# Global attention in steps of three half-column passes over six score banks

## The chip, the core and the metric

The kernel runs on one core of a Trainium2 chip. The metric is the device time of one execution in microseconds; the median of several runs is compared. Engines are named as the profile names them: PE is TensorE's matrix multiply, PEld its weight load, DVE is VectorE, ACT is ScalarE, POOL is GpSimd, SP is SyncE, which issues most transfers.

## The reference, cut to what matters

For each of 8 images of 64 x 64 tokens with 256 channels, two layers follow each other. The first is attention in windows of 512 tokens, 4 heads of 32 in horizontal windows (channels 0 to 127) and 4 in vertical ones (channels 128 to 255), plus a depthwise 3 x 3 convolution. The second is attention over all 4096 tokens with one head of 32; the change is in that one.

```python
# layer 2, tokens xf of one image, N = 4096, d = 32
f = xf @ kf + bf
g = xf @ kg + bg
h = xf @ kh + bh
s = jnp.einsum('bnd,bmd->bnm', g, f)
beta = jax.nn.softmax(s, axis=-1)
v = jnp.einsum('bnm,bmd->bnd', beta, h)
o = v @ kv + bv
out = gamma[0] * o.reshape(B, H, W, C) + x
```

## The kernel before, in words

**Units and steps.** The work is a list of units: per image 8 horizontal windows (`h0` to `h7`), 8 vertical ones (`v0` to `v7`) and two global units (`l0`, `l1`), each of which treats half of the queries as four blocks of 512. The first horizontal unit of the next image stands ahead of the two global units. A window unit has 4 steps, a global unit 32, one for each block of 128 keys (a tile).

One step does, for four blocks at once: scores, exponential, values, sum.

- `scores(c)` (L860 in global units, L679 in windows): four matmuls with 32 rows each, one in each row group of TensorE, 128 keys by 512 queries. The matmuls are fp32 and each stands as two instructions in the trace. The outputs are two bank pairs `s` of `[128, 2, 512]`, that is four PSUM banks. Three pairs exist, and `sc_tiles` hands out two of them in turn, so that one pair is free when the next step begins.
- `weights_of` (L477): two exponentials on ScalarE, one per pair, into the weights `p_l` (tag `pt`, three buffers).
- `weighted(c)` (L876): four matmuls, one in each column group, add into `num_l`. It is issued one step later, behind the next step's scores.
- `add(c)` (L887): VectorE adds the weights into `acc_l`, `[128, 4, 512]`; after the last step a matmul with ones (`sums`, L896) makes the denominators, `norm` (L904) divides and `result` (L915, and L262 through `product`) makes the output, which L925 evicts.

**Filler.** Between values and the next scores TensorE is given other work in half-width pieces: the projections of the next image (`pq`, L262), `pf` and `phd` for the global layer, and sums. VectorE and ScalarE have filler too: the convolution's taps (L618 on ScalarE, the other eight L622 on VectorE), evictions, hard-swish (L597, L604) and transposes.

**Order.** All of it stands in an order made by a planner (`Flow`) while the program is built. It keeps a clock for TensorE, ScalarE, VectorE and SyncE from fixed costs, and picks tasks by due times (`DUE`, in steps relative to a unit). Each engine then runs its own list in that order, and waits on semaphores. SyncE's list holds the loads of `x`, the round trips `kvia` and `via_v` through DRAM, and the outputs.

**GpSimd.** It has little to do: `clip` clears the border of an image part `hv` (L589 to L595) and `swish` copies two halo rows between neighbours (L609, L610).

A second program path with exact maxima stands behind a test of the denominators and is not taken with these inputs.

Of the kernel before, what the change touches and what calls it, by code (L numbers as in the profile page):

```python
# [18 lines left out]
P = 128  # L19
C = 256  # L20
H = W = 64
N = H * W
# [9 lines left out]
def quad(r):  # L32
# [3 lines left out]
HALVES = 2  # L36
QH = 4

DUE = dict(
    near_k=-4, near_q=-3, near_values=-13, clip=-2, swish=4,  # L40
    conv_h0=13, conv_h1=10, conv_h2=7, conv_h3=16, conv_v0=-3, conv_v1=-3, conv_v2=14, conv_v3=9,
    tap=-5, join_h=14, join_hl=10, join_v=12, context=0, norm=2, release=0, sums=-2, add=1, adds_h=0, adds_v=0, add2=1, apart=4,
    fg0=-7, fg2=11, fg3=20, h0=3, h1=14, values_v=-3, near0=3, spread0=12, spread1=61,
    conv_first=-10, far_swish=1,
# [7 lines left out]
SCORES, VALUES, PROD, TURN, DRAIN = 0.96, 0.88, 0.86, 0.65, 0.11  # L52
# [3 lines left out]
ISSUE, LOAD, VIA, FETCH, HALO = 0.6, 4.3, 2.6, 2.8, 2.6  # L56
# [20 lines left out]
class Flow:  # L77
# [5 lines left out]
    def __init__(self):  # L83
        self.t = 0
        self.clock = dict(pe=0.0, act=0.0, dve=0.0, sp=0.0)
        self.lanes = dict(pe=[], turn=[], act=[], dve=[], sp=[], res=[])
        self.open = None
        self.held = None
        self.bank_free = 0.0
        self.half_end = self.exp_end = 0.0  # L90
        self.apart = 0
# [116 lines left out]
    def step(self, scores, values):  # L208
        c = self.clock
        self.apart += 1  # L210
# [8 lines left out]
        if scores:  # L219
            scores()  # L220
            c["pe"] = max(c["pe"] + DRAIN, self.half_end + LAG) + SCORES
            self.half_end = max(c["act"], c["pe"] + PE_LAG) + EXP
# [12 lines left out]
        if self.held:  # L235
            self.held()
            c["pe"] = max(c["pe"] + DRAIN, before + LAG) + VALUES
        self.held = values
# [4 lines left out]
        for task in self.waiting("sp"):  # L243
            if task.begin() <= self.clock["pe"] + 0.5:
                self.run(task)
# [20 lines left out]
def tile_attention_blocks(  # L266
# [19 lines left out]
    B = xT.shape[0]  # L286
    PSUM = bass.MemoryType.PSUM
# [115 lines left out]
    seen = [const.tile([P, 2 * NB + 2, TB // D], F32, name=f"seen{i}") for i in range(2)]  # L403
    for t in seen:
        nc.gpsimd.memset(t, 1.0)

    def attention(images, load_x, out_rows, exact):


# [21 lines left out]
        pairs = cycle([ps_sc.tile([P, 2, TB], F32, name=f"s_{i}") for i in range(3)])  # L431
# [36 lines left out]
        def sc_tiles():  # L468
            return [next(pairs), next(pairs)]
# [49 lines left out]
        def image(b):  # L519
# [8 lines left out]
            def note():  # L528
                for t, op in zip(seen, (ALU.max, ALU.min)):
                    nc.vector.tensor_tensor(t, t, recs(), op)  # L530
# [50 lines left out]
            def clip(i, half):  # L581


                if i % 2 == 0:
# [4 lines left out]
                    nc.gpsimd.memset(v[:, :, 0:1], 0.0)  # L589
                    nc.gpsimd.memset(v[:, :, W + 1 : W + 2], 0.0)  # L590
                v = hv[i // 2, half]
                if i == 0:
                    nc.gpsimd.memset(v[:, 0, :], 0.0)
                if i == NB - 1:
                    nc.gpsimd.memset(v[:, 17, :], 0.0)  # L595
# [5 lines left out]
            def swish(i, half):  # L601
# [4 lines left out]
                )  # L606
                if i and i % 2 == 0:
                    here, before = hv[i // 2, half], hv[i // 2 - 1, half]
# [222 lines left out]
            def global_unit(z):  # L831
# [22 lines left out]

                def scores(c):
                    if exact and c == 0:
                        maxima()
                    sc = sc_tiles()
                    for r in range(NQ):
                        nc.tensor.matmul(  # L860
                            row_of(sc, r), lhsT=f4[quad(r), c * P : (c + 1) * P],
                            rhs=gq[quad(r), z, :], start=True, stop=not exact,
                        )
                        if exact:
                            row = slice(r * D, r * D + 1)
                            nc.tensor.matmul(
# [467 lines left out]
```

## Time and profile before

| | us |
|---|---|
| median of 3 runs | 3437.23 (3435.89 to 3438.12) |
| the profiled execution's own time | 3432.03 |
| its span, first to last instruction | 3430.1 |
| TensorE busy | 3368.3 (98%) |
| VectorE busy | 2729.4 (80%) |
| ScalarE busy | 2666.5 (78%) |
| GpSimd busy | 63.1 (2%) |
| granted TensorE clock | 0.997 |

In time, one image takes about 421 us: some 227 us of window units and 194 us of global units, in the middle of the run. Busy time of TensorE counts a matmul from its start to a modelled end, and an instruction that waits inside a group of matmuls isn't seen as idle time; starts are the firmer measure. Columns of a timeline: start, length, engine, line, operation, output and inputs, shape, count, and in brackets the idle time before it and what ended that.

### The profile page before, as it was taken

How to read it: one execution, taken by the hardware profiler on the slowest of the kernel's cores; microseconds unless marked ns; L12 is line 12 of the kernel's file. 1: busy time of each engine (PE TensorE's matmuls, PEld its weight loads, DVE VectorE, ACT ScalarE, POOL GpSimd, SP SyncE). 2: the span in 40 equal slices, each digit the busy share in tenths (PEclk: the TensorE clock that was granted, in tenths of full speed). 3: DMA queues.
4: the chain of work that ended last, by engine and by line, in shares of the span. 5: the costliest groups of instructions: out<-in, count | busy, mean ns of one | idle time of the engine just before them, and what ended most of it. 6: DMA issues, size and time to landing. Idle time of an engine off the chain costs nothing.

```text
span 3430.1 us, 80125 instructions
## 1 busy us (share of the span) xinstructions
PE 3368.3 (98%) x34804; PEld 1154.6 (34%) x34804; DVE 2729.4 (80%) x2276; ACT 2666.5 (78%) x3235; POOL 63.1 (2%) x266
## 2 busy tenths in 40 slices
PE   8999999999999999999999999999999999999997
PEld 3333333333333333333333333333333333333322
DVE  4897798777897778968789687896878968788776
ACT  5788777887787877878778787787877878778875
POOL 0000000000000000000000000000000000000000
PEclk9999999999999999999999999999999999999998
DMA  2131103311123111231112311123111231122200
GB/s 71 57 99 51 56 28 88 96 46 50 44 72 100 48 45 44 72 106 41 50 50 75 98 37 47 56 81 92 40 38 59 84 86 40 38 72 65 70 31 26
DMA packets 249417, 209.94 MB, mean 61 GB/s; under 512 B 26080, under 2 KB 190432, under 8 KB 249056
## 3 DMA queue, kind: packets, MB, share of 16 engines
q1 hardware_dynamic: 246816, 204.18, 20.4%
q8 instruction: 275, 4.51, 0.6%
q10 hardware_dynamic: 2240, 0.56, 0.1%
q14 instruction: 86, 0.70, 0.1%
HBM read 99.78 MB, written 83.89 MB: 54 GB/s over the span
## 4 chain that ended last, share of the span: by engine, by line
PE 79%; DVE 14%; ACT 4%; issue 2%; DMA 1%; DVEq 0%; ACTq 0%; SPq 0%
PE s L679 16%; DVE acc_l L887 12%; PE pq L262 11%; PE s L860 10%; PE num_l L876 8%; PE num_v L696 7%; PE num_h L696 7%; PE s L262 6%; PE sum_h L714 5%; PE sum_v L714 5%; PE pf L783 2%; DVE act L622 1%; ACT p_l L477 1%; ACT p_h L477 1%; PE s L915 1%
## 5 line engine op out<-in xcount | busy, mean ns | idle before, releaser
L887 DVE TENSOR_TENSOR acc_l<-acc_l,p_l 128x2048 f32<-128x2048 f32 x480 | 1099.8, 2291 | 230.7 <-ACT p_l L477 207.6
L477 ACT ACTIVATE p_l<-s 128x1024 f32<-128x1024 f32 x1024 | 992.9, 1026 | 200.6 <-PE s L860 143.7
L622 DVE SCALAR_TENSOR_TENSOR act<-hv,dw_sb,act 128x1024 f32<-128x1024 f32 x512 | 655.7, 1281 | 22.7 <-ACT act L618 8.6
L860 PE MATMUL s<-gq,f 32*128 32x512 f32 x4096 | 625.9, 640 | 1.4 <-ACT ot_l L925 0.9
L477 ACT ACTIVATE p_h<-s 128x1024 f32<-128x1024 f32 x512 | 494.5, 1023 | 94.9 <-PE s L679 70.9
L477 ACT ACTIVATE p_v<-s 128x1024 f32<-128x1024 f32 x512 | 496.0, 1023 | 92.7 <-PE s L679 86.9
L876 PE MATMUL num_l<-p_l,h_sb 128*32 128x512 f32 x4096 | 546.4, 605 | 2.4 <-ACT nums_l L891 2.1
L262 PE MATMUL pq<-x,wqkv_sb 128*32 128x256 f32 x8192 | 524.0, 382 | 2.1 <-ACT qh L551 0.8
L262 PEld LDWEIGHTS pq<-x,wqkv_sb 128*32 128x32 f32 x8192 | 261.3, 110 | 368.9 <-issue 201.9
L679 PE MATMUL s<-qh,kh 32*128 32x512 f32 x2048 | 319.0, 641 | 10.3 <-ACT qh L551 5.9
L679 PE MATMUL s<-qv,kv 32*128 32x512 f32 x2048 | 317.7, 640 | 0.2 <-ACT p_v L477 0.2
L860 PEld LDWEIGHTS s<-gq,f 32*128 32x128 f32 x4096 | 192.9, 182 | 298.6 <-issue 284.7
L696 PE MATMUL num_v<-p_v,vs 128*32 128x512 f32 x2048 | 272.7, 605 | 2.5 <-DMA vs<-kvia 2.5
L696 PE MATMUL num_h<-p_h,vs 128*32 128x512 f32 x2048 | 271.6, 602 | 3.5 <-ACT nums_l L891 1.9
L262 PE MATMUL s<-act,wout_sb 128*32 128x512 f32 x2048 | 227.0, 595 | 0.0
L925 ACT ACTIVATE ot_l<-s,bias_o 128x512 f32<-128x512 f32 x128 | 81.2, 684 | 174.2 <-PE s L262 162.7
L876 PEld LDWEIGHTS num_l<-p_l,h_sb 128*32 128x32 f32 x4096 | 80.7, 108 | 387.5 <-issue 370.7
L705 DVE TENSOR_TENSOR acc_h<-p_h,p_h 128x2048 f32<-128x2048 f32 x64 | 146.5, 2290 | 44.1 <-ACT p_h L477 30.9
L705 DVE TENSOR_TENSOR acc_v<-p_v,p_v 128x2048 f32<-128x2048 f32 x64 | 146.6, 2291 | 36.8 <-ACT p_v L477 36.8
L679 PEld LDWEIGHTS s<-qh,kh 32*128 32x128 f32 x2048 | 97.1, 183 | 182.2 <-issue 146.7
L679 PEld LDWEIGHTS s<-qv,kv 32*128 32x128 f32 x2048 | 101.6, 182 | 162.2 <-issue 157.9
L714 PE MATMUL sum_h<-p_h,ones 128*32 128x256 f32 x2048 | 137.3, 380 | 4.2 <-ACT kv L570 4.2
(125 smaller groups left out, 2417.8 us busy)
## 6 DMA issues: line engine op xcount, KB each, us to landing
x<-in_xT SPq DMA_DIRECT2D x92, 512.0 KB, 3.9
kvia<-kt SPq DMA_DIRECT2D x128, 256.0 KB, 2.4
vs<-kvia SPq DMA_DIRECT2D x512, 64.0 KB, 2.1
out<-ot_l SPq DMA_DIRECT2D x128, 256.0 KB, 2.1
via_v<-nums_v SPq DMA_DIRECT2D x64, 256.0 KB, 2.1
shuf_v<-via_v SPq DMA_DIRECT2D x256, 64.0 KB, 2.0
f<-fg SPq DMA_DIRECT2D x256, 64.0 KB, 2.0
gq<-fg SPq DMA_DIRECT2D x64, 64.0 KB, 2.0
```

What stands on the lines that cost most here:

```text
L262: nc.tensor.matmul(out[quad(r), :], lhsT=lhsT[:, quad(r)], rhs=rhs, start=start, stop=stop)
L477: nc.scalar.activation(pt[:, 2 * z : 2 * z + 2, :], sc[z], AF.Exp, scale=scale)
L622: nc.vector.scalar_tensor_tensor(o, src, wt, o, ALU.mult, ALU.add)
L679: nc.tensor.matmul(row_of(sc, r), lhsT=k[quad(r), c * P : (c + 1) * P], rhs=q[quad(r), :], start=True, stop=not exact,)
L696: nc.tensor.matmul(u["num"][quad(r), :], lhsT=vs[kind, i][:, r, c, :], rhs=u[c][:, r, :], start=(c == 0), stop=(c == 3),)
L705: nc.vector.tensor_add(u["acc"], u["acc"] if c == 2 else u[0], u[c])
L714: nc.tensor.matmul(u["sum"][quad(r), cols], lhsT=ones[:, :D], rhs=pt[:, r, cols], start=(k == 0), stop=(k == len(of) - 1),)
L783: nc.tensor.matmul(pf[quad(r), cols], lhsT=wcomb[:, k, quad(r % 2)], rhs=act_of(2 * p + r // 2, k, cols), start=(k == 0), stop=(k == 1),)
L860: nc.tensor.matmul(row_of(sc, r), lhsT=f4[quad(r), c * P : (c + 1) * P], rhs=gq[quad(r), z, :], start=True, stop=not exact,)
L876: nc.tensor.matmul(u["num"][quad(r), :], lhsT=h_sb[:, c, :], rhs=u[c][:, r, :], start=(c == 0), stop=(c == 4 * NB - 1),)
L887: nc.vector.tensor_add(u["acc"], u["acc"], u[c])
L925: nc.scalar.activation(ot, po, AF.Identity, bias=bias_o[:, m : m + 1])
```

## The change

The first two tiles of a global unit keep the old step. The other 30 are treated as 60 half-column passes, a pass being one tile against one half (256) of the query columns, and three passes make a step: 2 + 20 steps in place of 32. A step takes all three bank pairs: `first`, `mid` and `last`. Row groups 0 and 1 write `first` in passes one and two and `mid` in pass three; row groups 2 and 3 write `mid` in pass one and `last` in passes two and three. The next step gets the pairs in the order first, last, mid.

The pair `mid` is so written by different row groups in passes one and three. Between them stands a hand-over: an empty GpSimd instruction waits for pass one's last matmul, and pass three's first matmul waits for that instruction.

Three exponentials follow, the third (`mid`) into a tile `pm` of its own with one buffer. Values are three passes of four matmuls. VectorE adds twice per step, `add` for four half pairs and `add_rest` for `mid`.

The borders and halo copies of `hv` become tasks of their own (`edges`) in a new GpSimd lane, placed when VectorE's part is at least `BEHIND` = 3.0 us past by the planner's clock. Due times are set anew, some orders between tasks are changed, and the notes on denominators (`seen`) are kept per image.

```diff
 DUE = dict(
-    near_k=-4, near_q=-3, near_values=-13, clip=-2, swish=4,
-    conv_h0=13, conv_h1=10, conv_h2=7, conv_h3=16, conv_v0=-3, conv_v1=-3, conv_v2=14, conv_v3=9,
-    tap=-5, join_h=14, join_hl=10, join_v=12, context=0, norm=2, release=0, sums=-2, add=1, adds_h=0, adds_v=0, add2=1, apart=4,
-    fg0=-7, fg2=11, fg3=20, h0=3, h1=14, values_v=-3, near0=3, spread0=12, spread1=61,
-    conv_first=-10, far_swish=1,
+    near_k=-4, near_q=-2, near_values=-13, clip=6, swish=4,
+    conv_h0=12, conv_h1=10, conv_h2=6, conv_h3=18, conv_v0=-3, conv_v1=-5, conv_v2=16, conv_v3=9,
+    tap=-5, join_h=12, join_hl=13, join_v=12, context=0, norm=-6, release=0, sums=-2, add=1, adds_h=0, adds_v=0, add2=9, apart=-5,
+    fg0=-10, fg2=8, fg3=12, h0=1, h1=4, values_v=-3, near0=0, spread0=8, spread1=41,
+    conv_first=-13, far_swish=2,
 )
...
         if scores:
-            scores()
-            c["pe"] = max(c["pe"] + DRAIN, self.half_end + LAG) + SCORES
-            self.half_end = max(c["act"], c["pe"] + PE_LAG) + EXP
+            rest = scores()
+            c["pe"] = max(c["pe"] + DRAIN, self.half_end + LAG) + SCORES + more
+            self.half_end = max(c["act"], c["pe"] - more + PE_LAG) + EXP
+            if more:
+                self.half_end = max(self.half_end, c["pe"] + PE_LAG) + EXP
...
+        for task in self.waiting("pool"):
+            if task.begin() + BEHIND <= self.clock["pe"]:
                 self.run(task)
...
+                    first, mid, last = sc = [pairs.popleft() for _ in range(3)]
+                    pairs.extend((first, last, mid))
+                    for n, (tile, h) in enumerate(passes_of(c)):
+                        for r in range(NQ):
+                            mm = score(place_of(c, n, r, sc), r, tile, side(h))
+                            if n == 0 and r == 3:
+                                relay = nc.gpsimd.nop()
+                                handed(relay, mm)
+                            if n == 2 and r == 0:
+                                handed(mm, relay)
+                    pt = ptp.tile([P, NQ, TB], F32, tag="pt", name=name)
+                    nc.scalar.activation(pt[:, :2, :], first, AF.Exp)
+                    nc.scalar.activation(pt[:, 2:, :], last, AF.Exp)
+
+                    def rest():
+                        pm = ptp.tile([P, 2, TB], F32, tag="pm", name=f"{name}_m", bufs=1)
+                        nc.scalar.activation(pm, mid, AF.Exp)
+                        u[c] = pt, pm
...
+                    pt, pm = u[c]
+                    for n in (0, 2, 1):
+                        tile, h = passes_of(c)[n]
+                        for r in range(NQ):
+                            nc.tensor.matmul(
+                                u["num"][quad(r), side(h)], lhsT=h_sb[:, tile, :],
+                                rhs=place_of(c, n, r, (pt[:, :2], pm, pt[:, 2:])),
+                                start=False, stop=(c == l_steps - 1 and n == 1),
+                            )
...
+                def add_rest(c):
+
+                    h = passes_of(c)[0][1]
+                    acc = u["acc"].rearrange("p (j i) c -> p i j c", j=2)[:, :, :, side(h)]
+                    nc.vector.tensor_add(
+                        acc, acc, u[c][1].rearrange("p i (j c) -> p i j c", j=2)
+                    )
...
+                    if i % 2 == 0 or i == NB - 1:
+                        edges[i, half] = flow.add(
+                            "pool", [(partial(im.edges, i, half), [("pool", HALO)])], due, [sw[i, half]]
+                        )
...
+            def then():
+                if c - 1 in u.added:
+                    flow.require(u.added[c - 1])
+                rest()
```

## The prediction

> **What bounds the kernel now.** I read the busy table first, then the costliest groups, then the timeline of one global step with filler and of some without. From the page, parts 1 and 5:
>
> ```profile
> PE 3368.3 (98%) x34804; PEld 1154.6 (34%) x34804; DVE 2729.4 (80%) x2276; ACT 2666.5 (78%) x3235; POOL 63.1 (2%) x266
> ...
> L887 DVE TENSOR_TENSOR acc_l<-acc_l,p_l 128x2048 f32<-128x2048 f32 x480 | 1099.8, 2291 | 230.7 <-ACT p_l L477 207.6
> L477 ACT ACTIVATE p_l<-s 128x1024 f32<-128x1024 f32 x1024 | 992.9, 1026 | 200.6 <-PE s L860 143.7
> ...
> L860 PE MATMUL s<-gq,f 32*128 32x512 f32 x4096 | 625.9, 640 | 1.4 <-ACT ot_l L925 0.9
> ...
> L876 PE MATMUL num_l<-p_l,h_sb 128*32 128x512 f32 x4096 | 546.4, 605 | 2.4 <-ACT nums_l L891 2.1
> ```
>
> TensorE looks like the only bound. The timeline of an image's global stage, TensorE alone, starts of groups in the first column:
>
> ```profile
> 1624.29 1.14 PE L860 MATMUL s<-gq,f 32*128 32x512 f32 x8
> 1625.36 1.07 PE L876 MATMUL num_l<-p_l,h_sb 128*32 128x512 f32 x8
> 1626.24 1.05 PE L262 MATMUL pq<-x,wqkv_sb 128*32 128x256 f32 x16
> 1627.22 1.14 PE L860 MATMUL s<-gq,f 32*128 32x512 f32 x8
> ```
>
> Start to start, scores take 1.07 us, values 0.88 (1.00 where scores follow at once), and 16 half-width instructions of filler 0.98. Within scores the second four start 0.534 after the first four, within values 0.454; in filler each four of 256 columns take 0.216. So 512 columns take 0.427, and the rest is turning round: 0.107 of weights in the open plus 0.11 of emptying for scores, 0.027 plus 0.113 for values. A global step without filler is 2.07 us, of which 0.357 is turning.
>
> The other view, the last image's stage, where filler has run out:
>
> ```profile
> 3370.13 1.94 ACT L477 ACTIVATE p_l<-s 128x1024 f32<-128x1024 f32 x2 [0.46 <-DVE acc_l L887]
> 3370.14 9.48 DVE L887 TENSOR_TENSOR acc_l<-acc_l,p_l 128x2048 f32<-128x2048 f32 x4
> ...
> 3372.52 1.94 ACT L477 ACTIVATE p_l<-s 128x1024 f32<-128x1024 f32 x2 [0.46 <-DVE acc_l L887]
> 3373.25 0.64 PEld L860 LDWEIGHTS s<-gq,f 32*128 32x128 f32 x8 [0.84 <-issue]
> 3373.26 1.47 PE L860 MATMUL s<-gq,f 32*128 32x512 f32 x8
> ...
> 3375.65 0.64 PEld L860 LDWEIGHTS s<-gq,f 32*128 32x128 f32 x8 [0.84 <-issue]
> 3375.65 1.47 PE L860 MATMUL s<-gq,f 32*128 32x512 f32 x8
> ```
>
> Here steps start 2.40 apart, not 2.07: four dependent adds take 9.48, so one comes every 2.396 (2.292 plus 0.104 until its own result is visible), the exponentials wait for VectorE, and scores (now 1.40 long) wait inside. TensorE still counts as busy. **VectorE is the bound wherever a step has little filler.** Three weight buffers hide this for about ten tiles after filler ends; then 2.40 sets in. From starts over the whole trace I sum 135 us of such stretching: 4.8 in each of six global stages of 194.2 us, 6.2 in the seventh, 12.1 in the last, the rest mostly in window stages.
>
> **What the Trainium skill says.** "TensorE: Matmul & The Clock Gate", section "LDWEIGHTS (loading the stationary operand)", has load time go by columns, not rows: the trace agrees, 0.107 exposed for 128 columns and 0.027 for 32. "TensorEngine Tiling (Array Packing)", section "Gotcha 1: PSUM Pressure", says row tiles may not write one bank at the same time and software must order them: the reason for the hand-over; nothing run so far shows a collision. "PSUM — Partial Sum Buffer", section "Engine vs sequencer instructions", puts a nop on the sequencer alone, so the hand-over needs no GpSimd datapath, but its queue is a strict FIFO. The trace supports the price: wait-only instructions take 17 ns (ScalarE) and 21 ns (VectorE).
>
> **The change, part by part.** The order of the built program gives the counts.
>
> *Turns.* Per half image, 2 full steps and 20 of three passes replace 32, so 160 fewer score/values pairs over 16 halves: 160 x 0.357 = 57.1 us off. A 256-column pass costs 0.432 against 0.427: 320 steps x 6 passes x 0.0045 = 8.6 back. Doubled weight loads lie under streaming (0.107 against 0.216); if not, each is worth up to 0.1 us. Net 48.5 off; pricing every group in both orders gives 48.6 (51.6 in global stages, 3.0 back in window stages).
>
> *Step length.* Three passes: scores 0.107 + 6 x 0.216 + 0.11 = 1.51, values 1.44, together 2.95 us, for 1.5 tiles (3.10 before).
>
> *Adds.* Per step a 128x2048 add and a 128x1024 one. The trace's 2.292 (2048) and 0.69 (512) give 1.22 for 1024. Both are in the chain on `acc`: 2.292 + 1.22 + 2 x 0.104 = **3.72 us per step** against 1.5 x 2.396 = 3.59. That exceeds 2.95, and what lets VectorE trail shrinks: the middle pair's weights have one buffer, so the third exponential of step k waits for the second add of k-1, and (third bank pair) the second pass of k+1 waits for that exponential. All six banks belong to one step. Three exponentials, 0.92 apart, then cost nothing more: about 3.3 per step, under 3.72.
>
> *Filler.* In the new order a middle image's global stage has 11 three-pass steps without filler, 7 with 0.4 to 0.6 us, 7 with about 1.2, 13 with 1.4 to 1.9, and 2 with 9.9 (results). Taking the later of TensorE and VectorE step by step, the 11 gain 9.7 us of wait (VectorE 42.2, TensorE 32.5), the 7 gain 5.6, the rest about 4. Full-filler neighbours can absorb lateness of about 1.1 us; following it through by hand leaves 12.7 per stage, against 4.8 now: +7.9, times 7 = +55. Bounds: 4.8 (no worse than now) and 19.3 (nothing absorbed). So bare work falls 6.5 per stage and waits rise 7.9.
>
> *Last image.* 36 of its 40 three-pass steps have no filler. At 3.72 the stage takes about 165 us. Before it took 169.3 with two results tasks (16.1) inside. In the new order these two come after the last step, the normalisation feeding them standing behind the adds on VectorE. Of their 16.1, 9.3 falls into gaps where TensorE now idles (4.2 before L896, 5.1 from L896 to L915). Net 165 + 16.1 - 9.3 - 169.3 = +2.5; the turns above already count -6.1 of it, so +8.6.
>
> *Hand-over.* Row group 3 of pass one streams until 0.56 us after the step's start; a result is visible 0.21 after streaming (scores at 1624.29, exponential at 1625.46, streaming ending 0.96 in). Wait-only instruction 0.02, back to TensorE 0.05 (exponential end to weight load in the tail), weights 0.107: 0.95, and pass three may start at 0.97. Just hidden: lower bound 0; it removes no wait, so no gain. Upper, 0.15 late: 320 x 0.15 = 48. Queued behind the waiting matmul are pass three and all later TensorE work; ScalarE's second and third exponentials wait for it. I take 3.
>
> *GpSimd's queue.* Today it stands waiting for VectorE up to 165 us at a time, harmless as no engine is near it. Now a hand-over could stand behind such a copy. The new `edges` tasks are placed 3 us after planned readiness, and in global stages cost 3.35 us of GpSimd work. Taken 0; upper 20 in all.
>
> *Window stages.* Re-tuned due times move filler, taps and joins, and the DMAs of `fetch_values` and `load` with them, past others on SP. VectorE gets about 5 us more per image there (4.5 of its work moves out of the global stage). The summed later-of-TensorE-and-ScalarE rises 1.9 per stage. I take +1 x 7 = +7, from -15 to +20. The one memset fewer and the smaller `seen` reductions: nothing (VectorE slack).
>
> Sum: -48.6 + 55 + 8.6 + 3 + 7 = **+25 us**. Against the profiled execution's 3432.0 (span 3430.1 plus 1.9) that is 3457; the median of the runs is 5.2 above it, so 3462.
>
> **Rivals.**
> 1. *The banks and buffers cover it; faster.* One mechanism: in the 18 low-filler steps per stage, VectorE's lateness is taken up by filled neighbours and waits stay at 4.8 per stage. Then -48.6 plus a few: about 3391. It decides below 11.3 us of wait per stage (4.8 + 6.5). For: the present stage's later-of sum is 17 us above TensorE, yet only 4.8 is lost. Against: that relies on three buffers, and the middle pair now has one. Chance 0.26.
> 2. *Balance.* Waits come to some 10 us per stage and window stages don't grow: 3437. Chance 0.10.
> 3. *The hand-over is late.* 0.15 per step, or copies ahead of it in GpSimd's queue: 48 to 68 on top of my sum, 3510 to 3530. Chance 0.06.
> The change not doing what it says is excluded: the new order shows the half-column passes and a TensorE wait on GpSimd's sequencer in each step.
> My forecast, VectorE pacing the low-filler steps, has 0.58.
>
> **How the numbers follow.** My own case runs 3440 to 3500. The range 3405 to 3500 adds balance and the upper half of rival 1, leaving out its lower half and rival 3, about 0.2. Within 0.2% (6.9 us) is about what measurement here can't tell from no change. Faster 0.26, same 0.10, slower 0.64.
>
> **What would show it.** Right: three-pass steps without filler start about 3.7 apart, not 2.95; the third exponential waits for `acc_l`; VectorE without gaps there; global stages 195 to 199 us. Hand-over: the weight load of pass three with no wait on GpSimd, pass one to pass three 0.86 apart. Wrong: global stages near 188, or a tail below 3.4 per step, or idle time put down to GpSimd.

## The result, and the profile after

The changed kernel takes 3461.98 us (median of 4 runs, 3461.68 to 3464.65), the kernel before 3436.56 beside it: ratio 1.0077, 95% interval 1.0060 to 1.0094. The profiled execution took 3462.07 us, its span 3460.3. The forecast was 3462.0.

Lines of the page after that answer to those shown of before (line, engine, operation; busy us and mean ns; idle time before, and what ended most of it):

```profile
PE 3393.1 (98%) x42484; PEld 1519.6 (44%) x42484; DVE 2753.7 (80%) x2436; ACT 2686.8 (78%) x3235; POOL 62.9 (2%) x264
...
L983 DVE TENSOR_TENSOR acc_l<-acc_l,p_l 128x2048 f32<-128x2048 f32 x320 | 733.1, 2291 | 203.6 <-ACT p_l L947 189.5
...
L989 DVE TENSOR_TENSOR acc_l<-acc_l,p_l_m 128x1024 f32<-128x1024 f32 x320 | 392.1, 1225 | 33.5 <-DVE acc_l L983 0.5
L951 ACT ACTIVATE p_l_m<-s 128x1024 f32<-128x1024 f32 x320 | 329.2, 1029 | 74.2 <-DVE acc_l L989 70.6
```

480 additions of 2.29 us have become 320 of 2.29 and 320 of 1.225: per tile VectorE now has more to do. The third exponential, L951, waits 70.6 us in all for the middle addition. The waits of the whole trace (us, times, longest) show who passes this on:

```profile
PEld s L901 <- ACT p_l_m L951: 89.7, 198, 2.5
...
ACT p_l_m L951 <- DVE acc_l L989: 70.6, 155, 1.8
...
PEld s L901 <- ACT p_l L947: 41.1, 99, 0.8
```

In the trace of before, weight loads of the global scores waited 7.0 us for exponentials in all. The timeline of one step without filler, late in an image's global stage (start, length):

```profile
895.79 2.36 PE L901 MATMUL s<-gq,f 32*128 32x256 f32 x24
895.94 1.02 ACT L951 ACTIVATE p_l_m<-s 128x1024 f32<-128x1024 f32 x1 [0.44 <-DVE acc_l L989]
895.95 2.29 DVE L983 TENSOR_TENSOR acc_l<-acc_l,p_l 128x2048 f32<-128x2048 f32 x1
...
897.02 0.73 PEld L901 LDWEIGHTS s<-gq,f 32*128 32x128 f32 x12 [0.50 <-ACT p_l_m L951]
...
898.35 1.23 DVE L989 TENSOR_TENSOR acc_l<-acc_l,p_l_m 128x1024 f32<-128x1024 f32 x1
...
899.51 2.37 PE L901 MATMUL s<-gq,f 32*128 32x256 f32 x24
899.67 1.02 ACT L951 ACTIVATE p_l_m<-s 128x1024 f32<-128x1024 f32 x1 [0.44 <-DVE acc_l L989]
```

VectorE runs L983, L989, L983 with 0.10 us between them. The third exponential starts 0.09 us after L989 ends, and the second half of pass two starts when that exponential has freed its bank. Scores last 2.29 us to the first values instead of 1.51, and the step 3.72 instead of 2.95.

By place, from the starts of the global scores (us; "middle" is the median of the seven stages before the last, from first to last scores; "windows" is the sum of the seven stretches between global stages; "tail" runs from the last scores to the end). These columns come from each kernel's one profiled execution, which lay 4.5 us under the median for before and 10.4 under it for e3_no_triples:

| kernel | median | first global stage begins | middle | windows | last stage | tail |
|---|---|---|---|---|---|---|
| before | 3436.6 | 285.6 | 193.7 | 1577.3 | 168.2 | 41.6 |
| after | 3462.0 | 294.1 | 195.8 | 1578.1 | 169.7 | 47.2 |
| e1_buffer | 3466.0 | 296.3 | 192.9 | 1603.0 | 171.1 | 41.9 |
| e2_narrow | 3412.8 | 295.1 | 191.1 | 1579.1 | 153.2 | 46.9 |
| e3_no_triples | 3498.0 | 295.9 | 193.7 | 1621.3 | 169.2 | 40.8 |
| e4_due | 3537.7 | 291.4 | 196.3 | 1637.3 | 186.4 | 46.3 |
| e5_shared_buffer | 3445.9 | 294.6 | 193.3 | 1582.2 | 171.5 | 41.9 |
| e6_triples_only | 3474.6 | 287.4 | 196.4 | 1592.1 | 170.9 | 46.1 |
| e7_edits_only | 3464.1 | 295.1 | 193.7 | 1597.9 | 169.3 | 41.3 |
| e8_late_relay | 3463.1 | 293.2 | 195.8 | 1580.2 | 170.6 | 47.3 |
| e9_relay_memset | 3484.2 | 293.3 | 198.9 | 1578.7 | 170.6 | 47.3 |
| e10_narrow_both | 3365.4 | 292.9 | 185.9 | 1579.5 | 144.1 | 46.7 |
| e11_first_image | 3438.3 | 286.8 | 192.9 | 1583.5 | 172.7 | 42.4 |
| e12_tuned | 3420.0 | 285.9 | 193.1 | 1563.1 | 171.5 | 41.5 |

From before to after the span grows by 30.2 us: 8.5 ahead of the first global stage, 13.8 in the seven middle stages, 0.8 in the windows between, 1.5 in the last stage and 5.6 in the tail.

### The profile page after: what moved, and what is told of

Same layout as the page of the kernel before. It is cut to its first block, busy times and chain, and to the rows that moved or that the text cites. A ratio compares the mean times of both kernels' runs of the same rounds, so it can differ in the third digit from the quotient of the medians.

```text
span 3460.3 us, 95984 instructions
## 1 busy us (share of the span) xinstructions
PE 3393.1 (98%) x42484; PEld 1519.6 (44%) x42484; DVE 2753.7 (80%) x2436; ACT 2686.8 (78%) x3235; POOL 62.9 (2%) x264
## 4 chain that ended last, share of the span: by engine, by line
PE 84%; DVE 10%; ACT 3%; issue 1%; DMA 1%; DVEq 0%; SPq 0%; ACTq 0%
PE s L723 17%; PE pq L283 13%; PE s L901 11%; PE num_l L970 9%; PE num_v L740 7%; PE num_h L740 7%; PE s L283 6%; DVE acc_l L983 6%; PE sum_v L758 5%; PE sum_h L758 5%; DVE acc_l L989 3%; PE pf L827 2%; PE s L1019 1%; PE phd L854 1%; DVE act L666 1%
## 5 line engine op out<-in xcount | busy, mean ns | idle before, releaser
L983 DVE TENSOR_TENSOR acc_l<-acc_l,p_l 128x2048 f32<-128x2048 f32 x320 | 733.1, 2291 | 203.6 <-ACT p_l L947 189.5
L901 PE MATMUL s<-gq,f 32*128 32x256 f32 (+1 forms) x7936 | 652.5, 408 | 19.3 <-ACT p_l_m L951 6.5
L901 PEld LDWEIGHTS s<-gq,f 32*128 32x128 f32 x7936 | 408.3, 184 | 266.3 <-issue 93.6
L283 PE MATMUL pq<-x,wqkv_sb 128*32 128x256 f32 x8192 | 505.8, 382 | 3.6 <-ACT qv L595 1.7
L970 PE MATMUL num_l<-p_l,h_sb 128*32 128x256 f32 x5120 | 481.9, 382 | 0.0
L989 DVE TENSOR_TENSOR acc_l<-acc_l,p_l_m 128x1024 f32<-128x1024 f32 x320 | 392.1, 1225 | 33.5 <-DVE acc_l L983 0.5
L951 ACT ACTIVATE p_l_m<-s 128x1024 f32<-128x1024 f32 x320 | 329.2, 1029 | 74.2 <-DVE acc_l L989 70.6
L946 ACT ACTIVATE p_l<-s 128x1024 f32<-128x1024 f32 x320 | 327.6, 1024 | 51.5 <-PE s L901 48.3
L947 ACT ACTIVATE p_l<-s 128x1024 f32<-128x1024 f32 x320 | 328.4, 1026 | 26.4 <-PE s L901 23.2
L970 PE MATMUL num_l<-p_l_m,h_sb 128*32 128x256 f32 x2560 | 332.6, 385 | 0.7 <-ACT p_l_m L951 0.7
L970 PEld LDWEIGHTS num_l<-p_l,h_sb 128*32 128x32 f32 x5120 | 205.5, 110 | 165.9 <-issue 110.8
```

The source lines that it names most:

```text
L283: nc.tensor.matmul(out[quad(r), :], lhsT=lhsT[:, quad(r)], rhs=rhs, start=start, stop=stop)
L901: mm = nc.tensor.matmul(po, lhsT=f4[quad(r), tile * P : (tile + 1) * P], rhs=gq[quad(r), z, cols], start=True, stop=not exact,)
L947: nc.scalar.activation(pt[:, 2:, :], last, AF.Exp)
L951: nc.scalar.activation(pm, mid, AF.Exp)
L970: nc.tensor.matmul(u["num"][quad(r), side(h)], lhsT=h_sb[:, tile, :], rhs=place_of(c, n, r, (pt[:, :2], pm, pt[:, 2:])), start=False, stop ...
L983: nc.vector.tensor_add(u["acc"], u["acc"], pt)
```

## The experiments

**What holds the three-pass steps: VectorE's middle addition.**

```diff
-    acc, acc, u[c][1].rearrange("p i (j c) -> p i j c", j=2)
+    acc[..., :4], acc[..., :4],
+    u[c][1].rearrange("p i (j c) -> p i j c", j=2)[..., :4],
```

> The changed kernel with its middle addition cut to 16 of its 1024 columns (4 of each run of 256): the order of all instructions stays, VectorE does 1.1 us less in each three-pass step. The global denominators lack nearly all of the middle pair's part.
> Theory (VectorE's chain): a step asks VectorE for about 2.3 + 0.2 + 0.15 = 2.65 us, less than the 2.95 of TensorE. Steps without filler lie 2.95-3.1 us apart instead of 3.72, the middle global stages come to 184-186 us instead of 195.8, the last to 150-156 instead of 169.7: 3462 - 7 x 11 - 16 = 3369 us, between 3355 and 3390.
> Rival A (hand-over): no change, 3462 +- 4.
> Rival B (ScalarE): its three exponentials of 1.03 us keep steps without filler at 3.3 us or more, stages about 190, 3415 us.

3412.78 us, ratio 0.9931 (0.9916 to 0.9946). The middle stages come to 191.1 only, and steps without filler in a row to 3.24 and 3.34 by turns, in the last stage as well. That is rival B's number; that the last stage, at 153.2 us, falls in the theory's range says little, since its steps are not the theory's 2.95 to 3.1. Two of those steps in the timeline of this kernel:

```profile
889.45 2.29 DVE L983 TENSOR_TENSOR acc_l<-acc_l,p_l 128x2048 f32<-128x2048 f32 x1 [0.84 <-ACT p_l L947]
...
890.72 1.03 ACT L946 ACTIVATE p_l<-s 128x1024 f32<-128x1024 f32 x1 [0.39 <-PE s L901]
891.64 1.02 ACT L947 ACTIVATE p_l<-s 128x1024 f32<-128x1024 f32 x1
891.85 0.18 DVE L989 TENSOR_TENSOR acc_l<-acc_l,p_l_m 128x16 f32<-128x16 f32 x1
892.55 1.02 ACT L951 ACTIVATE p_l_m<-s 128x1024 f32<-128x1024 f32 x1
892.69 2.29 DVE L983 TENSOR_TENSOR acc_l<-acc_l,p_l 128x2048 f32<-128x2048 f32 x1 [0.67 <-ACT p_l L947]
...
894.06 1.02 ACT L946 ACTIVATE p_l<-s 128x1024 f32<-128x1024 f32 x1 [0.48 <-PE s L901]
```

VectorE now waits for exponentials, so it no longer leads. ScalarE runs three exponentials 0.92 apart and then waits for TensorE, which itself waits inside its scores for the bank that the third frees. So a second limit stands right behind VectorE's.

**ScalarE's third exponential as well.**

```diff
-    nc.scalar.activation(pm, mid, AF.Exp)
+    nc.scalar.activation(pm[..., :16], mid[..., :16], AF.Exp)
...
-    rhs=place_of(c, n, r, (pt[:, :2], pm, pt[:, 2:])),
+    rhs=place_of(c, n, r, (pt[:, :2], pt[:, :2], pt[:, 2:])),
```

> As e2_narrow, and the third exponential too is cut to 16 of 512 columns of each half; the values of the middle half-columns read the first pair's exponentials in its place, so the output is not the reference's there. ScalarE has about 0.9 us less in a three-pass step.
> Theory (what e2_narrow left, 3.24 us a step without filler, is ScalarE's turn: three exponentials of 1.03 us and the bank that the third hands to the next step): steps without filler lie 2.95 us apart, also behind one another; the middle global stages go from 191.1 to 185-187 us, the last from 153.2 to 149-151: 3412.8 - 7 x 5 - 3 = 3375 us, between 3362 and 3390.
> Rival (TensorE's own order, tiling switches and results tasks make up the rest): stages stay at 190-191 us, 3405-3413 us.

3365.35 us, ratio 0.9793 (0.9777 to 0.9810). Middle stages 185.9, as the theory has it; the last 144.1, below its 149. The timeline of this kernel, in the last stage:

```profile
3280.00 0.20 ACT L951 ACTIVATE p_l_m<-s 128x32 f32<-128x32 f32 x1
...
3280.15 1.58 PE L901 MATMUL s<-gq,f 32*128 32x256 f32 x24
...
3283.09 1.79 PE L901 MATMUL s<-gq,f 32*128 32x256 f32 x24
...
3286.25 0.93 PE L901 MATMUL s<-gq,f 32*128 32x256 f32 x12
```

Steps lie 2.94 and 3.16 us apart by turns. The first is TensorE's own; in the second the scores are 0.21 longer, so a wait is left inside every other step, where the theory wanted 2.95 throughout. A narrow exponential also lets most of its bank go without a wait; that part isn't told apart from ScalarE's time. Of a middle stage's 195.8 us, then, 4.7 go with the middle addition and 5.2 more with the third exponential; of the last stage's 169.7, 16.5 and 9.1. These shares hold for this order: the third exponential was not cut alone, with the middle addition whole.

**A second buffer for the third exponential,** in two forms. In both, the third exponential of a step stands behind the additions of two steps before, no longer behind those of the step before.

```diff
-    pm = ptp.tile([P, 2, TB], F32, tag="pm", name=f"{name}_m", bufs=1)
+    pm = ptp.tile([P, 2, TB], F32, tag="pm", name=f"{name}_m", bufs=2)
...
-CTX = 4
+CTX = 3
...
-    kt = work.tile([P, TB], F32, tag="kt", name=f"kt_{b}_{kind}_{i}")
+    kt = work.tile([P, TB], F32, tag="kt", name=f"kt_{b}_{kind}_{i}", bufs=1)
```

> The changed kernel with a second buffer for the third exponential's tile p_l_m, so that the third exponential of a step needs the middle addition of two steps before, not of the one before. Room for it comes from one buffer less for h contexts (4 to 3) and for turned values (2 to 1); those are used in the window stages, which must then stay at 227 us.
> Theory (VectorE's chain of dependent additions, 3.72 us a step, ends last in the steps without filler, and one buffer passes each of these on to TensorE at once): a single short step is now absorbed, a row of them is not. The seven middle global stages go from 195.8 to 190-192 us, the last from 169.7 to 160-166; steps in a row without filler still lie 3.72 apart. Time 3462 - 7 x 4.5 - 6 = 3425 us, between 3415 and 3437.
> Rival A (the bank hand-over through GpSimd sets the waits): nothing moves, 3462 +- 4 us.
> Rival B (ScalarE, with three exponentials of 1.03 us and the evictions in its queue, ends last): at most the part that waits behind add is gone, steps without filler come below 3.5 us also in a row, stages 194-196.

3465.99 us, ratio 1.0086 (1.0073 to 1.0100). The middle stages fall to 192.9 as expected, the last doesn't, and the window stages, which were to stay, give more than that back: 1603.0 against 1578.1. A wait of this kernel's third window stage that the changed kernel doesn't have, VectorE ahead of the turned values:

```profile
DVE kt L676 <- DMA kvia<-kt: 6.5, 4, 2.7
```

The room for the buffer had been taken from tiles in use. How much of the loss is this tile's, and how much that of the contexts (`CTX`), isn't told apart. So the same edit again, with its room taken from nobody:

```diff
-    pm = ptp.tile([P, 2, TB], F32, tag="pm", name=f"{name}_m", bufs=1)
+    pm = work.tile([P, 2, TB], F32, tag="kt", name=f"{name}_m")
...
-    kt = work.tile([P, TB], F32, tag="kt", name=f"kt_{b}_{kind}_{i}")
+    claim(None)
+    kt = work.tile([P, 2, TB], F32, tag="kt", name=f"kt_{b}_{kind}_{i}")[:, 0, :]
```

> The changed kernel with two buffers for the third exponential's tile, this time with no buffer taken from the window stages: p_l_m (4 KB a partition) takes turns with the tile kt of turned values in two buffers of 4 KB, in place of one for p_l_m and two of 2 KB for kt; each new tile first has the additions issued that read the tile two before.
> Theory (e1_buffer gained 2.9 us a middle stage and lost it again in the window stages, where its single kt waited for transfers): middle global stages 192-194 us, window stages 227 +- 1.5, last stage 168-171: 3462 - 7 x 2.8 = 3442 us, between 3434 and 3452.
> Rival (sharing moves the wait: in the last dozen steps of a stage the third exponential now waits for the transfer out of kt): middle stages 195-198, 3455-3475 us.

3445.92 us, ratio 1.0032 (1.0020 to 1.0044). Middle stages 193.3, windows 1582.2. The tail is 5.3 shorter than after, as two results tasks stand inside the last stage again; that comes from the new order, not from the buffer. The waits of this kernel answer to those of after:

```profile
PEld s L902 <- ACT p_l_m L952: 58.4, 145, 0.9
...
ACT p_l_m L952 <- DVE acc_l L990: 23.5, 54, 0.8
```

89.7 us have become 58.4, and 70.6 have become 23.5. One buffer was worth about 2.5 us a stage. In a row of steps without filler, 3.73 now sets in late: in the last stage most such steps lie 3.17 and 3.41 apart by turns. Their mean, 3.29, is that of the 3.24 and 3.34 in e2_narrow, so the second limit stands behind the buffers too.

**The hand-over.** The first form puts six more empty GpSimd instructions behind the first.

```diff
     handed(relay, mm)
+    for _ in range(6):
+        relay = nc.gpsimd.nop()
```

> The changed kernel with six more empty GpSimd instructions behind the first in each bank hand-over, all in line; pass three waits for the last of the seven.
> Theory (the hand-over is hidden with only some 0.02 us to spare): pass two to pass three, now 0.216 us where nothing else waits, grows by what six empty instructions take[...] in the 200 steps or so that do not wait for VectorE or ScalarE anyway: 3462 + 30 to 70 = 3492-3530 us.
> Rival (there is more slack than worked out, or the empty instructions overlap): pass three stays 0.216 behind, 3462 +- 4 us.

3463.10 us. The built program has none of the six (its trace has 320 empty instructions, one for each hand-over): it is the changed kernel again and says nothing of the hand-over, only that one program repeats within 1.7 us per stage. The second form uses an instruction that does something.

```diff
     handed(relay, mm)
+    relay = nc.gpsimd.memset(pause, 0.0)
```

> The changed kernel with a real GpSimd instruction in each bank hand-over: behind the empty one, GpSimd clears a tile of its own (128 x 64), and pass three waits for that. (In e8_late_relay the six further empty instructions had no wait and no waiter of their own and are not in the built program; it ran the changed kernel's own instructions.)
> Theory (the hand-over is hidden with some 0.02 us to spare): the clearing takes about as long as the edge clearings of this kernel, 0.13-0.15 us, and its dispatch and semaphore come on top; pass two to pass three goes from 0.216 to 0.33-0.5 us in the steps that wait for nothing else, about 200 of 320: 3462 + 25 to 55 = 3487-3517 us.
> Rival (the slack is larger): pass three stays 0.216 behind, 3462 +- 4 us.

3484.20 us, ratio 1.0142 (1.0125 to 1.0159), just under the expected range. All instances of that tile, and who waited for them:

```profile
L944 POOL MEMSET pause<- x320: 151/151/154, 302.0 to 3434.1; 128x64 f32 x160
...
who waited for it (us, times):
  PEld s L902: 51.2, 157
```

Take the steps that wait for nothing else, with times from the step's first matmul. In the changed kernel the empty instruction runs from 0.782 to 0.799, the first weight load of pass three starts at 0.850, 0.051 behind it, and the two halves of pass three start at 0.967 and 1.183. Here the clearing runs from 0.867 to 1.018, and that load starts at 1.069, again 0.051 behind. The load is 0.219 later, and the second half of pass three, at 1.391, is 0.208 later: all but 0.011 of the lateness comes through, so about 0.01 was to spare. The halves are 0.320 apart in place of 0.216 because the load of the first half, 0.104, is now in the open, as it is in pass one of every step. The middle stages pay 3.1 us each. The last stage, which VectorE holds, takes 170.6 us, as with e8_late_relay.

**Where the 8.5 us ahead of the first global stage come from.** First, all but the three-pass steps, with the due times of before:

```diff
-FULL = 2
+FULL = N // P
...
-    near_k=-4, near_q=-2, near_values=-13, clip=6, swish=4,
+    near_k=-4, near_q=-3, near_values=-13, clip=-2, swish=4,
...
-    u.ends.append(flow.add("res", pieces, u.t + u.steps + 3 * m, [u.normed], im.ends[-1:]))
+    u.ends.append(flow.add("res", pieces, u.t + u.steps + 4 * m, [u.normed], im.ends[-1:]))
```

> The changed kernel with no three-pass step at all (the number of two-pass steps set to all 32 of a unit) and with the due times and result spacing of the kernel before: what is left of the change are the GpSimd edge instructions as tasks of their own, the dropped clearing of edges, the reuse of conv buffers across images, and the shorter note of the sums.
> Theory (these edits cost nothing, all of the loss is in three-pass steps and due times): 3437 us, between 3432 and 3441; first global stage begins at 285.6 us, middle stages 193.7, last 168, tail 41.6.
> Rival (they hold 8 us of the loss, by edge instructions that now come late and hold a conv or a context in the first image): first global stage begins at 290-295 us, 3444-3448 us in all.

3497.96 us, ratio 1.0182 (1.0168 to 1.0196): neither theory nor rival. The global stages are those of before, the start is the rival's, but the window stages lose another 44 us. Step by step, the third stretch runs as in before to within 0.02 us until 101 us from its start, at the end of unit `h6`, and has lost 7.9 some 14 us later, at the end of `h7`. The timelines of ScalarE and TensorE there, in this kernel:

```profile
1448.91 2.85 ACT L518 ACTIVATE p_h<-s 128x1024 f32<-128x1024 f32 x3 [3.24 <-DVE acc_h L749]
...
1458.15 1.94 ACT L518 ACTIVATE p_h<-s 128x1024 f32<-128x1024 f32 x2 [3.57 <-PE s L723]
```

```profile
1449.98 2.08 PE L723 MATMUL s<-qh,kh 32*128 32x512 f32 x4 [2.00 <-ACT p_h L518]
```

An exponential stands 3.24 us behind an addition that VectorE reaches late, and TensorE waits 2.00 for it. Then the granted clock is 0.50 for 6.8 us (1449.7 to 1456.5), and matmuls take nearly twice as long; eight matmuls of values in this kernel and, below, in before:

```profile
1451.99 1.94 PE L740 MATMUL num_h<-p_h,vs 128*32 128x512 f32 x8
```

```profile
1423.86 1.06 PE L696 MATMUL num_h<-p_h,vs 128*32 128x512 f32 x8
```

The window stages between the images of before have no such half clock. Here the wait of 2.00 stands in all seven stretches. In two of them 6.8 us of half clock follow, and they take 235.2 and 235.3 us; in three 3.4 us follow, and they take 233.7 to 234.0; in two none does, and of these the full-length one takes 232.8. So of the 7.9 us lost in the third stretch about 2.4 go with the clock, and the rest with another order of the same work. Which edit brings that order isn't told apart: beside the moved edge work, this kernel has the reuse of conv buffers across images and the shorter notes on denominators.

Then the due times of the window stages alone, in the changed kernel:

```diff
-    near_k=-4, near_q=-2, near_values=-13, clip=6, swish=4,
-    conv_h0=12, conv_h1=10, conv_h2=6, conv_h3=18, conv_v0=-3, conv_v1=-5, conv_v2=16, conv_v3=9,
+    near_k=-4, near_q=-3, near_values=-13, clip=-2, swish=4,
+    conv_h0=13, conv_h1=10, conv_h2=7, conv_h3=16, conv_v0=-3, conv_v1=-3, conv_v2=14, conv_v3=9,
...
```

> The changed kernel, three-pass steps and all, with the due times of the window stages from the kernel before (near_q, clip, conv_h, conv_v, join_h, join_hl, norm, add2); those of the global stages (fg, h, spread, near0, apart, conv_first, far_swish) stay as changed.
> Theory (the first global stage begins 8.5 us later because of the re-tuned due times): it begins at 285-288 us instead of 294.1, the window stages between later images stay within 1.5 us of 227 each, middle global stages 195.8 +- 0.5: 3462 - 7 = 3455 us, between 3448 and 3462.
> Rival (the start comes from other edits, such as edges done by tasks on GpSimd, or the due times were needed by the three-pass stages): the first global stage begins at 292 us or later, or it begins early and the later window stages give it back, 3460-3470 us.

3537.68 us, ratio 1.0297 (1.0283 to 1.0311). The start gains only 2.7; the windows lose 59 and the last stage 17. The theory is wrong, and the rival right in kind, but the loss is far above its 3460 to 3470. In the window stages between images TensorE is at half clock for 44 us in all, against 3.4 in the changed kernel. In the last stage nearly all of the loss stands in one step, that of the last projections (L827): 27.87 us, against 12.12 in the changed kernel. TensorE waits there 3.13 and then 9.38 us for VectorE, VectorE waits 5.89 of these for a round trip through DRAM (`via_v`), and from the end of the first wait on the clock is at half for 13.7 us. Then each half of the change alone:

```diff
-    "dve", [(partial(im.swish, i, half), [("dve", SWISH)])],
+    "dve", [(partial(im.swish, i, half), [("dve", SWISH), ("dma", HALO)])],
...
-    if i % 2 == 0 or i == NB - 1:
-        edges[i, half] = flow.add(
-            "pool", [(partial(im.edges, i, half), [("pool", HALO)])], due, [sw[i, half]]
-        )
```

> The three-pass steps alone: the window side of the kernel before is put back (clearing of edges ahead of clip, edge copies behind swish, conv waits within the image, and the window due times near_q, clip, conv_h, conv_v, join_h, join_hl, norm, add2); the three-pass steps and the changed due times of the global stages stay.
> Theory (the 8.5 us at the start come from the moved edge work, which the re-tuned window due times make good in the later images only; the three-pass steps cost 2.1 us a stage and the longer tail): first global stage begins at 285-287 us, window stages 227-229, middle global stages 195-196.5, last 170, tail 47: 3453 us, between 3447 and 3465.
> Rival (the window due times were needed by the shorter step count of a global stage, as in e4_due): window stages 232-235, last stage 185, 3510-3540 us.

3474.57 us, ratio 1.0117 (1.0101 to 1.0132): outside both ranges. The start is at 287.4, close to the theory's 285 to 287, and the middle stages are at 196.4, as it has them; but the windows take 14 us more than after in all.

```diff
-FULL = 2
+FULL = N // P
...
-    fg0=-10, fg2=8, fg3=12, h0=1, h1=4, values_v=-3, near0=0, spread0=8, spread1=41,
+    fg0=-7, fg2=11, fg3=20, h0=3, h1=14, values_v=-3, near0=3, spread0=12, spread1=61,
```

> No three-pass step at all, as in e3_no_triples, but with the changed kernel's due times for the window stages (near_k to norm, add2) beside the moved edge work; the due times of the global stages are those of before.
> Theory (moved edge work and re-tuned window due times belong together): first global stage begins at 293-295 us, window stages 226-229, global stages 193.7: 3437 + 8.5 = 3445 us, between 3440 and 3453.
> Rival (these due times fit only a global stage of 44 steps, not one of 64): window stages 230 or more, 3465 us or more.

3464.09 us, ratio 1.0083 (1.0069 to 1.0097). The start is late again, 295.1, without a single three-pass step: the edge work and its due times are what the first image pays for. The windows take 1597.9 where the theory wanted 1587 at most (six of 229, one of 213) and after has 1578.1; that is nearer the rival. In no kernel here that lacks one of the three, steps, edge work or due times, do the window stages come back to 227 us.

The clock plays a small part in the 8.5 us. Ahead of the first global stage TensorE is at half clock for 10.2 us in the changed kernel and never in before. But e10_narrow_both, whose instructions up to there are those of the changed kernel, has 3.4 us of it and begins at 292.9, and e7_edits_only has 3.4 too and begins at 295.1.

**Both repairs, and a version that beats both kernels.** The first image's window stage gets its old form back, on top of the shared buffer:

```diff
+FIRST = DUE | dict(near_k=-4, near_q=-3, clip=-2, swish=4, conv_h0=13, conv_h1=10, conv_h2=7,
+    conv_h3=16, conv_v0=-3, conv_v1=-3, conv_v2=14, conv_v3=9, tap=-5, join_h=14, join_hl=10, join_v=12)
...
+    if (exact or b == images[0]) and (i % 2 == 0 or i == NB - 1):
+        edges(i, half)
...
-    if i % 2 == 0 or i == NB - 1:
+    if not n:
+        edges[i, half] = sw[i, half]
+    elif i % 2 == 0 or i == NB - 1:
```

> e5_shared_buffer with the first image's window stage put back to the form of before: there the edge work is done at once behind swish again, and near_q, clip, conv_h, conv_v, tap, join_h, join_hl and join_v have their due times of before. Later images are as in e5_shared_buffer.
> Theory (the 8.5 us before the first global stage come from the moved edge work and the due times tuned for later images, where filler is there to fill the gaps): the first global stage begins at 286-288 us instead of 294.6, all else stays: 3446 - 7.5 = 3438 us, between 3433 and 3442.
> Rival (the first image's loss comes from the three-pass steps' planning): it still begins at 292 us or later, 3446 us.

3438.25 us, ratio 1.0011 (1.0004 to 1.0018). The first global stage begins at 286.8, and the rest stays: the theory's number. With both repairs the three-pass steps come out level with the two-pass ones, no better. Last, other due times:

```diff
-    near_k=-4, near_q=-2, near_values=-13, clip=6, swish=4,
-    conv_h0=12, conv_h1=10, conv_h2=6, conv_h3=18, conv_v0=-3, conv_v1=-5, conv_v2=16, conv_v3=9,
-    tap=-5, join_h=12, join_hl=13, join_v=12, context=0, norm=-6, release=0, sums=-2, add=1, adds_h=0, adds_v=0, add2=9, apart=-5,
...
+    near_k=-4, near_q=2, near_values=-13, clip=6, swish=4, conv_h0=14, conv_h1=10, conv_h2=4, conv_h3=18, conv_v0=-3, conv_v1=-7, conv_v2=16, conv_v3=8, tap=-8, join_h=15, join_hl=12, join_v=11, context=6, norm=-9, release=0, sums=-2, add=7, adds_h=0, adds_v=0, add2=11, apart=-5, fg0=-10, fg2=9, fg3=10, h0=2, h1=4, values_v=-3, near0=-5, spread0=8, spread1=43, conv_first=-13, far_swish=5,
```

> A version meant to beat both kernels: e11_first_image with other due times (near_q 2, conv_h0 14, conv_h2 4, conv_v1 -7, conv_v3 8, tap -8, join_h 15, join_hl 12, join_v 11, context 6, norm -9, add 7, add2 11, fg2 9, fg3 10, h0 2, near0 -5, spread1 43, far_swish 5). They were picked by replaying each engine's built instruction list with the durations of the traces, an estimate that puts each window stage between images some 4 us below that of e11_first_image and leaves the global stages alone.
> Theory (with VectorE's and ScalarE's turns given, what is left to win is the order in the window stages): window stages 223-226 us instead of 228, middle global stages 193-194, 3438 - 7 x 2.5 = 3420 us, between 3410 and 3432, below the kernel before.
> Rival (an order that good on paper is lost to waits that the replay doesn't know): 3435 us or more.

3420.01 us, ratio 0.9959 (0.9945 to 0.9972): faster than both, by 0.4% against before. Nearly all of the gain over e11_first_image lies in the window stages, 1563.1 against 1583.5. It is a gain of order, not of the three-pass steps, and whether the kernel before would gain as much from its own due times wasn't tried.

## Why the prediction was right or wrong

The number was right, 3462.0 against 3461.98, and the main mechanism too, but agreement to 0.02 us is luck. In the profiled executions the change adds 30.2 us to the span, not 25: they give 3462.07 where the sum gives 3457. The forecast then added the 5.2 us by which the profiled execution of before lay under its median; that of the changed kernel lies at its own median, and the two fives cancel. The terms, too, are off in both directions.

- **Middle stages.** Forecast +9.8 in all (7.9 of wait less 6.5 of turns, seven times); measured +13.8. The signs for it were there as named: steps without filler in a row 3.72 apart, L951 waiting for `acc_l`, VectorE without gaps but for 0.10 us. The stages, 195.8, lie in the forecast 195 to 199.
- **The share of VectorE in it** is the step that was wrong. The prediction held three exponentials to cost nothing more because 3.3 is under 3.72. In the row of about six steps without filler that ends each middle stage that is so. But other such steps stand alone, and behind each the next step takes 3.64 us without filler of its own, in the changed kernel (at 772.89) and in e2_narrow (at 768.60) alike. The timeline of the changed kernel there:

```profile
772.05 1.02 ACT L947 ACTIVATE p_l<-s 128x1024 f32<-128x1024 f32 x1
...
772.89 2.28 PE L901 MATMUL s<-gq,f 32*128 32x256 f32 x24
772.95 1.03 ACT L951 ACTIVATE p_l_m<-s 128x1024 f32<-128x1024 f32 x1
773.10 2.29 DVE L983 TENSOR_TENSOR acc_l<-acc_l,p_l 128x2048 f32<-128x2048 f32 x1 [0.53 <-ACT p_l L947]
774.03 0.73 PEld L901 LDWEIGHTS s<-gq,f 32*128 32x128 f32 x12 [0.42 <-ACT p_l_m L951]
```

  L951 follows L947 without a wait for VectorE, which is itself idle, and TensorE waits for the bank that L951 frees. So e2_narrow gets 4.7 us a stage and e10_narrow_both 5.2 more. What ends last in a long row isn't what ends last in a short one.
- **Buffers.** That the middle pair has only one buffer was named as the reason for which lateness gets through. A second is worth about 2.5 us a stage (e5_shared_buffer), a part of the 12.7 us of wait forecast. With it the stages are level with before, and long rows still take 3.29 a step in the mean. So rival 1, in which the banks and buffers cover the lateness, falls on the second limit too; a second buffer together with a shorter third exponential was not measured.
- **Last image.** Forecast +2.5, measured +7.1, of which the stage 1.5 and the tail 5.6. The stage was put at 165 and took 169.7 (the forecast has 169.3 for it before, this table 168.2, so the two aren't measured quite alike). e5_shared_buffer shows the tail's part to be the place of the two results tasks: back inside the stage, tail 41.9.
- **Windows.** Forecast +10 (7, and 3 of turns given back), spread over all stages. Measured: +0.8 between the images and +8.5 ahead of the first. The size was near, the place not. e7_edits_only and e11_first_image show that the edge work and the due times of the changed kernel cost it in the first image. Why only there is argued and not shown: the first image has no previous image's global stage to work in.
- **Hand-over.** Forecast 3, with 0.02 us to spare; measured under 1, with 0.01 to spare, so its working was right step by step. In 157 of the 320 steps the load of pass three follows the empty instruction at once, and in 149 of these pass three still starts 0.216 behind pass two. Rival 3 is real as a mechanism: 0.22 later, it costs 22 us (e9_relay_memset), but it doesn't happen here. GpSimd's queue was put at nothing, and no cost shows: in none of these 157 steps does the empty instruction come more than 0.02 us later than usual.

What stays open: how much of the last stage's 4.7 us over the forecast each cause has. The trace of the changed kernel shows two. The last projections (half of `pf`, all of `phd` and `ph`) stand together in one step of 12.12 us, where TensorE waits some 3.3 us for VectorE and ScalarE by turns; in before the same work is spread over five steps. And where the second unit begins, VectorE waits for the sums of the first, and three steps take 4.01, 4.20 and 5.68 us. The longest waits of the two places:

```profile
3287.00 1.49 PE L827 MATMUL pf<-act,wcomb 128*32 128x256 f32 x20 [1.45 <-DVE act L808]
...
3341.79 2.29 DVE L980 TENSOR_TENSOR acc_l<-p_l,p_l 128x2048 f32<-128x2048 f32 x1 [5.14 <-PE sum_l L1000]
```

## What to carry to other kernels

When work is taken off one engine, list for the same steps what every other engine needs, in a long row and for a step alone: here TensorE wants 2.95 us, ScalarE's turn some 3.3 and VectorE 3.72, and taking 0.15 off TensorE brought nothing in long rows without filler. Due times are part of the order they were tuned for: edits around cheap GpSimd work made a single window unit 8 us longer, more than the effect on a whole global stage, so compare by stage before believing a total. Compare the granted clock by stage as well: a mean of 0.993 over the run hid stretches at 0.50 just where time was lost. A buffer has to be paid for with one that stands idle at the time.

## What the runs showed of the hardware that was not expected

The granted clock can fall to half after a short wait: in e3_no_triples five of seven waits of 2.00 us were followed by 3.4 or 6.8 us at 0.50, which made the stretch about 1 or 2.4 us longer, and two were not. What decides it isn't shown here. The way from TensorE over an empty GpSimd instruction and back fits into a pass with almost nothing to spare: the instruction takes 0.017, the weight load starts 0.051 behind it, and a load 0.219 later delayed the matmuls behind it by 0.208. And VectorE overlaps independent instructions by about 0.085 us (a 128x2048 addition and the next instruction start 2.20 apart for a length of 2.29, in the trace of before), while one of these additions that reads the sum of the one before starts 0.104 after its end: 0.19 us lie between the two, twice in each three-pass step of a long row.
